# Attention over a graph: V as the stationary operand in two column halves, with probabilities normalised before they are transposed

## The chip, the cores and the metric

The kernel runs on one core of one Trainium2 chip. Times are device microseconds (us) of the core, from the first to the last instruction of one execution. The engines are PE (TensorE: products and transposes), PEld (PE's weight loads), DVE (VectorE), ACT (ScalarE), POOL (GpSimd) and SP (it issues the transfers).

## The reference, cut to what matters

Two layers of masked attention with residual and layer norm, in float32, over 128 batches of 128 tokens of 512 features. Layer 0 has 4 heads of 64, layer 1 has 8, and layer 1 normalises its input first.

```
sim  = einsum('bhid,bhjd->bhij', q, k) * scale      # layer 0: 4 heads; layer 1: 8 heads
sim  = where(mask, sim, neg)
attn = softmax(sim)                                 # over the last axis
out  = einsum('bhij,bhjd->bhid', attn, v)           # "attended values"
x    = layernorm(x + merge_heads(out) @ Wo + bo)
```

## The kernel before: the parts that matter

Four batches make a group, and there are 32 groups. A group's inputs are transposed and projected together to Q, K and V (PE alone). Then its four batches pass through five attention stages, one turn per batch; in one turn different batches stand in different stages. Layer 0 of group g alternates with layer 1 of group g - 1. A scheduler in the build decides the order on each engine from this program order.

```python
def scores(l, g, b):        # cut: products q k, masking on DVE, maximum on DVE
    for s in range(2):
        for k in range(H // 2):          # one exponential per head, on ACT, with its sum
            nc.scalar.activation(sm[:, s, k, :], sm[:, s, k, :], AF.Exp, bias=nmax[:, s, k:k + 1],
                                 accum_out=total[:, s, k:k + 1])

def probs_t(l, g, b):
    rec = three.tile([P, H // 2, 2], F32, ...)
    nc.vector.reciprocal(rec.rearrange("p k s -> p s k"), SUM[l, g, b])
    pT = two.tile([P, H, N], F32, ...)
    for h0 in range(0, H, 4):
        pt = tr_tile(...)                # a PSUM bank
        for h in range(h0, h0 + 4):      # exponentials, not yet divided, head by head
            nc.tensor.transpose(pt[:, (h - h0) * N:(h - h0 + 1) * N], sm[:, h % 2, h // 2, :], ident)
        ...                              # copied to pT by DVE (first four) or ACT

def attend(l, g, b):
    for h in range(H):                   # the exponentials are stationary, V moves (64 columns)
        nc.tensor.matmul(pm[:, h * D:(h + 1) * D], pT[:, h, :], v[:, b, h * D:(h + 1) * D],
                         start=True, stop=True)
    nc.vector.tensor_mul(a, pm, rec)     # cut: the division, while leaving PSUM

def attended_t(l, g, b):                 # `a` is transposed by PE, copied by ACT to aT
    ...

def residual(l, g, b):                   # cut: xb = x + bias (POOL), o = aT Wo (PE), y = o + xb, norm (DVE)
    ...

STAGES = (scores, probs_t, attend, attended_t, residual)

for g in range(NG + 1):                  # cut
    transposed(0, g, X[g]); project(0, g)
    for b in range(G):
        turn((0, g, b))
        if b == 1 and g > 0:
            h = prenorm(g - 1)           # the norm in front of layer 1
    transposed(1, g - 1, h); project(1, g - 1)
    for b in range(G):
        turn((1, g - 1, b))
```

## Time and profile before

| | before |
|---|---|
| time, median of 3 runs | 4096.69 us (4096.34 to 4097.61) |
| one group of four batches, from the trace | 126.28 us |
| of it layer 1: projections / attention | 42.43 / 30.03 us |
| of it layer 0: projections / attention | 21.08 / 32.74 us |
| PE idle in the profiled run | 4094.8 - 3890.9 = 203.9 us |

The group is cut where an attention stretch starts (the first output product `o` after the V projection) and where a projection starts (the first product `qk`). The prediction below cuts one stretch a little later, so its rows differ by one or two us.

### The profile page before, as it was taken

The numbers are of one execution on the slowest core, as the hardware profiler recorded it, in microseconds if no ns is written. First come the engines' busy times: TensorE is split into PE (matmuls) and PEld (weight loads), VectorE is DVE, ScalarE is ACT, GpSimd is POOL, SyncE is SP. The second block draws the span as 40 slices with busy tenths as digits, with TensorE's granted clock in tenths as the row PEclk, the third lists the DMA queues.
The fourth block names the chain that finished last, engine by engine and source line by source line (L and its number), as shares of the span: only waits on it lengthen the run. The fifth ranks groups of instructions, "written<-read, shape, count | busy, mean of one in ns | idle before, by whom it ended". The sixth has DMA issues, their size and how long they took to land.

```text
span 4094.8 us, 42881 instructions
## 1 busy us (share of the span) xinstructions
PE 3890.9 (95%) x16193; PEld 2270.6 (55%) x16193; DVE 1654.0 (40%) x3366; ACT 1139.0 (28%) x4013; POOL 755.3 (18%) x1095
## 2 busy tenths in 40 slices
PE   8999999999999999999999999999999999999998
PEld 5555555555555555555555555555555555555554
DVE  3343443434434334334344343443434434334443
ACT  2322322223323133232232222322313323223222
POOL 1121211212212112112121121221211211112120
PEclk8999999999999999999999999999999999999998
DMA  3000000000000000000000000000000000000000
GB/s 100 12 22 11 22 17 17 22 11 22 22 14 19 16 17 22 17 17 22 11 22 17 16 22 11 22 19 14 22 11 22 22 14 19 21 12 22 6 13 14
DMA packets 56894, 78.78 MB, mean 19 GB/s; under 512 B 19816, under 2 KB 21360, under 8 KB 56688
## 3 DMA queue, kind: packets, MB, share of 16 engines
q1 hardware_dynamic: 56688, 76.04, 5.4%
q8 instruction: 128, 2.10, 0.2%
q14 instruction: 78, 0.64, 0.1%
HBM read 42.47 MB, written 33.55 MB: 19 GB/s over the span
## 4 chain that ended last, share of the span: by engine, by line
PE 72%; DVE 13%; POOL 7%; ACT 4%; issue 3%; DMA 1%; POOLq 0%; ACTq 0%
PE qk L134 33%; PE v L148 16%; PE o L252 8%; PE av L211 4%; PE xt L118 3%; PE sc L170 3%; DVE sm L175 3%; ACT sm L182 3%; PE pt L196 3%; POOL rstd L239 3%; POOL xb L249 2%; DVE nmax L178 2%; POOL sm L173 2%; DVE h L271 1%; DVE y L255 1%
## 5 line engine op out<-in xcount | busy, mean ns | idle before, releaser
L134 PE MATMUL qk<-xT,w 128*128 128x512 f32 x3072 | 1364.2, 601 | 0.0
L134 PEld LDWEIGHTS qk<-xT,w 128*128 128x128 f32 x3072 | 582.1, 193 | 674.9 <-issue 665.1
L249 POOL TENSOR_TENSOR xb<-x,bias 128x512 f32<-128x512 f32 x256 | 324.4, 1267 | 2776.4 <-DVE x L255 1577.2
L252 PE MATMUL o<-wo,aT 128*128 128x512 f32 x1536 | 768.3, 630 | 2.6 <-ACT aT L226 1.8
L182 ACT ACTIVATE sm<-sm,nmax 128x128 f32<-128x128 f32 x1536 | 595.0, 390 | 462.5 <-DVE nmax L178 461.4
L148 PE MATMUL v<-w,xT 128*128 128x256 f32 (+1 forms) x2048 | 670.9, 486 | 0.0
L148 PEld LDWEIGHTS v<-w,xT 128*128 128x128 f32 x2048 | 389.1, 190 | 285.0 <-issue 260.2
L141 DVE COPY qk<-qk 128x512 f32<-128x512 f32 x96 | 66.4, 692 | 959.5 <-PE qk L134 959.5
L196 PE MATMUL pt<-ident,sm 128*128 128x128 f32 x1536 | 317.9, 306 | 124.5 <-ACT sm L182 122.3
L150 DVE COPY v<-v 128x512 f32<-128x512 f32 x192 | 132.8, 692 | 747.4 <-PE v L148 747.4
L226 ACT COPY aT<-at 128x256 f32<-128x256 f32 (+1 forms) x256 | 121.8, 476 | 1117.1 <-PE at L224 1116.6
L252 PEld LDWEIGHTS o<-wo,aT 128*128 128x128 f32 x1536 | 288.3, 203 | 253.4 <-issue 230.8
L211 PE MATMUL av<-v,pT 128*128 128x64 f32 x3072 | 378.2, 274 | 0.2 <-DVE pT L202 0.2
L211 PEld LDWEIGHTS av<-v,pT 128*128 128x128 f32 x3072 | 369.6, 195 | 1.2 <-DVE pT L202 0.9
L196 PEld LDWEIGHTS pt<-ident,sm 128*128 128x128 f32 x1536 | 202.0, 154 | 272.9 <-ACT sm L182 188.5
L170 PE MATMUL sc<-qk 64*128 64x128 f32 x3072 | 319.4, 299 | 1.7 <-DVE sm L175 1.7
L175 DVE COPY_PREDICATED sm<-m,sc 128x256 f32<-128x256 uint8 (+1 forms) x512 | 283.0, 574 | 39.1 <-PE sc L170 35.8
L182 ACT ACTIVATION_READ_ACCUMULATOR sm<-sm,nmax 128x1 f32 x1536 | 289.8, 189 | 0.0
L170 PEld LDWEIGHTS sc<-qk 64*128 64x128 f32 x3072 | 233.7, 187 | 57.4 <-issue 27.8
L173 POOL MEMSET sm<- 128x512 f32 (+1 forms) x256 | 197.9, 773 | 301.9 <-PE pt L196 301.6
L178 DVE TENSOR_REDUCE nmax<-sm 128x4 f32<-128x512 f32 (+1 forms) x256 | 240.8, 940 | 3.3
L137 ACT ACTIVATE qk<-qk 128x512 f32<-128x512 f32 x192 | 114.6, 597 | 424.5 <-PE qk L134 424.5
(45 smaller groups left out, 2217.4 us busy)
## 6 DMA issues: line engine op xcount, KB each, us to landing
x<-in_x_dram SPq DMA_DIRECT2D x32, 1024.0 KB, 5.3
out_dram<-y SPq DMA_DIRECT2D x128, 256.0 KB, 2.0
w_qkv<-in_L_gnn_w_qkv_dram SPq DMA_DIRECT2D x12, 256.0 KB, 2.7
m<-in_adj_dram SPq DMA_DIRECT2D x32, 64.0 KB, 2.1
w_out<-in_L_gnn_w_out_dram SPq DMA_DIRECT2D x4, 256.0 KB, 2.7
w<-in_L_gnn_Wq_dram SPq DMA_DIRECT2D x1, 512.0 KB, 6.4
w<-in_L_gnn_Wk_dram SPq DMA_DIRECT2D x1, 512.0 KB, 7.3
w<-in_L_gnn_Wv_dram SPq DMA_DIRECT2D x1, 512.0 KB
```

The costliest lines, as they stand in the source:

```text
L134: nc.tensor.matmul(pm, W[l][:, c, f * P:(f + 1) * P], xT[:, c, :], start=(c == 0), stop=(c == KC - 1))
L148: nc.tensor.matmul(pm[:, (b - b0) * I:(b - b0 + 1) * I], xT[:, c, b * N:(b + 1) * N], W[l][:, c, 2 * I:3 * I], start=(c == 0), stop=(c == ...
L150: nc.vector.tensor_copy(v[:, b0:b0 + per, :], pm.rearrange("p (b i) -> p b i", i=I))
L170: nc.tensor.matmul(ps[:, h % 2, h // 2, :], qk[r, h // 2, t], qk[r, H // 2 + h // 2, t], start=True, stop=True)
L173: nc.gpsimd.memset(sm, (NEG0, NEG1)[l])
L175: nc.vector.copy_predicated(sm[:, s], mask[:, None, :].to_broadcast([P, H // 2, N]), ps[:, s, :H // 2, :])
L178: nc.vector.tensor_reduce(nmax, sm, AX.X, ALU.max, negate=True)
L182: nc.scalar.activation(sm[:, s, k, :], sm[:, s, k, :], AF.Exp, bias=nmax[:, s, k:k + 1], accum_out=total[:, s, k:k + 1])
L196: nc.tensor.transpose(pt[:, (h - h0) * N:(h - h0 + 1) * N], sm[:, h % 2, h // 2, :], ident)
L211: nc.tensor.matmul(pm[:, h * D:(h + 1) * D], pT[:, h, :], v[:, b, h * D:(h + 1) * D], start=True, stop=True)
L249: nc.gpsimd.tensor_tensor(xb, xin, (bias0, bias1)[l], op=ALU.add)
L252: nc.tensor.matmul(pm, aT[:, c * P:(c + 1) * P], WO[l][:, c, :], start=(c == 0), stop=(c == nk - 1))
```

## The change

V becomes the stationary operand, so the product comes out transposed already: heads with even numbers write PSUM partitions 0 to 63, heads with odd numbers 64 to 127 (two column halves of the array). The transposes of attended values, `attended_t`, go. But queries now lie along the free axis, so the division by the row sum can no longer be done there; it moves ahead of the transposes of the probabilities, half of the heads on POOL and half on DVE.

```diff
     def probs_t(l, g, b):
-        rec = three.tile([P, H // 2, 2], F32, ...)
-        nc.vector.reciprocal(rec.rearrange("p k s -> p s k"), SUM[l, g, b])
+        rec = three.tile([P, 2, H // 2], F32, ...)
+        nc.vector.reciprocal(rec, SUM.pop((l, g, b)))
+        for s, eng in enumerate((nc.gpsimd, nc.vector)):
+            eng.tensor_tensor(sm[:, s], sm[:, s],
+                              rec[:, s, :, None].to_broadcast([P, H // 2, N]), op=ALU.mult)
 ...
     def attend(l, g, b):
         for h in range(H):
-            nc.tensor.matmul(pm[:, h * D:(h + 1) * D], pT[:, h, :], v[:, b, h * D:(h + 1) * D], ...)
-        nc.vector.tensor_mul(a, pm, rec)
-    def attended_t(l, g, b): ...
+            r = slice((h % 2) * D, (h % 2 + 1) * D)
+            nc.tensor.matmul(pm[r, h // 2 * N:(h // 2 + 1) * N], v[:, b, h * D:(h + 1) * D],
+                             pT[:, h, :], ...)
+        nc.scalar.copy(aT, pm[:, :I // P * N])
 ...
-    STAGES = (scores, probs_t, attend, attended_t, residual)
+    STAGES = (scores, probs_t, attend, residual)
```

More of the change, by code (lines that the diff above doesn't have):

```diff
@@ L151, in project @@
         QK[l, g], V[l, g] = qk, v
-    SM, PT, SUM, A, AT = {}, {}, {}, {}, {}
+    SM, PT, SUM, AT = {}, {}, {}, {}
     def scores(l, g, b):
@@ L188, in probs_t @@
         sm = SM.pop((l, g, b))
-        rec = three.tile([P, H // 2, 2], F32, tag="rec", name=f"rec{l}_{g}_{b}")
-        nc.vector.reciprocal(rec.rearrange("p k s -> p s k"), SUM[l, g, b])
-        SUM[l, g, b] = rec
+        rec = three.tile([P, 2, H // 2], F32, tag="rec", name=f"rec{l}_{g}_{b}")
+        nc.vector.reciprocal(rec, SUM.pop((l, g, b)))
+        for s, eng in enumerate((nc.gpsimd, nc.vector)):
+            eng.tensor_tensor(sm[:, s], sm[:, s],
+                              rec[:, s, :, None].to_broadcast([P, H // 2, N]), op=ALU.mult)
         pT = two.tile([P, H, N], F32, tag="pT", name=f"pT{l}_{g}_{b}")
@@ L207, in attend @@
         pT, v = PT.pop((l, g, b)), V[l, g]
-        rec = SUM.pop((l, g, b)).rearrange("p k s -> p (k s)")
         pm = mm_tile(f"av{l}_{g}_{b}")
         for h in range(H):
-            nc.tensor.matmul(pm[:, h * D:(h + 1) * D], pT[:, h, :], v[:, b, h * D:(h + 1) * D],
-                             start=True, stop=True)
-        a = two.tile([P, I], F32, tag="a", name=f"a{l}_{g}_{b}")
-        nc.vector.tensor_mul(a.rearrange("p (h d) -> p h d", d=D),
-                             pm[:, :I].rearrange("p (h d) -> p h d", d=D),
-                             rec[:, :, None].to_broadcast([P, H, D]))
-        A[l, g, b] = a
-    def attended_t(l, g, b):
-        I = INNER[l]
-        a = A.pop((l, g, b))
-        pt = tr_tile(f"at{l}_{g}_{b}")
-        for c in range(I // P):
-            nc.tensor.transpose(pt[:, c * P:(c + 1) * P], a[:, c * P:(c + 1) * P], ident)
-        aT = two.tile([P, I], F32, tag="aT", name=f"aT{l}_{g}_{b}")
-        nc.scalar.copy(aT, pt[:, :I])
+            r = slice((h % 2) * D, (h % 2 + 1) * D)
+            nc.tensor.matmul(pm[r, h // 2 * N:(h // 2 + 1) * N], v[:, b, h * D:(h + 1) * D],
+                             pT[:, h, :], start=True, stop=True)
+        aT = two.tile([P, I // P * N], F32, tag="aT", name=f"aT{l}_{g}_{b}")
+        nc.scalar.copy(aT, pm[:, :I // P * N])
         AT[l, g, b] = aT
```

## The prediction

> **What bounds the kernel now.** I read the busy line of the page first, then the chain that ended last, then busy time by stretch of one group of four batches, then the groups by shape, last the timeline of TensorE (PE).
>
> ```profile
> PE 3890.9 (95%) x16193; PEld 2270.6 (55%) x16193; DVE 1654.0 (40%) x3366; ACT 1139.0 (28%) x4013; POOL 755.3 (18%) x1095
> ...
> PE 72%; DVE 13%; POOL 7%; ACT 4%; issue 3%; DMA 1%; POOLq 0%; ACTq 0%
> ```
>
> PE is busy for 95% of the span, yet only 72% of the chain lies on it; 24% lies on DVE, POOL and ACT. So some stretches are tied to PE's work and others to a chain over the other engines, which PE happens to fill. One group shows which (columns: stretch, its length, then busy us of PE, PEld, DVE, ACT, POOL, the clock, DMA):
>
> ```profile
> 1503.10:1545.50 42.40, 42.40 (x102) 18.90 (x101) 3.75 (x7) 6.74 (x17) 0.00 (x0) 0.98 0.00 0
> 1545.50:1577.00 31.50, 29.22 (x186) 20.32 (x185) 23.38 (x44) 15.47 (x66) 11.05 (x16) 0.95 0.12 36
> 1577.00:1596.60 19.60, 19.60 (x63) 11.62 (x62) 1.59 (x3) 4.33 (x14) 0.00 (x0) 1.00 0.00 1
> 1596.60:1629.40 32.80, 29.59 (x160) 19.45 (x159) 22.75 (x52) 8.80 (x31) 12.54 (x18) 0.97 0.08 32
> ```
>
> A group takes 126.3 us. Rows one and three are the projections of layer 1 and layer 0: PE alone, 62 us, untouched by the change. Rows two and four, 64.3 us, are attention, and there DVE is busy for 46.1 us (72%). Everything the change touches lies in these two rows. PE's only large wait is there too:
>
> ```profile
> PE pt L196 <- ACT sm L182: 122.3, 93, 2.6
> ```
>
> 122 of PE's 204 idle us (4094.8 - 3890.9) are transposes of probabilities waiting for their exponentials.
>
> ```profile
> 1548.87 1.16 PE L170 MATMUL sc<-qk 64*128 64x128 f32 x16
> 1549.96 1.98 PE L252 MATMUL o<-wo,aT 128*128 128x512 f32 x4
> ...
> 1567.18 0.63 PE L224 MATMUL at<-ident,a 128*128 128x128 f32 x4
> 1567.65 1.90 PE L211 MATMUL av<-v,pT 128*128 128x64 f32 x16
> 1569.48 1.16 PE L170 MATMUL sc<-qk 64*128 64x128 f32 x14
> ```
>
> From start to start: 4 transposes `at` take 0.47 us (0.12 each), 16 `av` passes 1.83 us (0.114 each), 16 score passes 1.09 us (0.068 each, entry and exit included). Every float32 product is two passes: 3072 `av` records for 12 heads x 128 batches = 1536 products.
>
> **What the Trainium skill says.** "TensorE: Matmul & The Clock Gate", section LDWEIGHTS, gives a weight load as columns / 1.2 ns, so 107 ns for 128 columns. The trace agrees: `av` moves only 64 columns and still takes 114 ns a pass, so it is paced by its 128-column load. "TensorEngine Tiling (Array Packing)", Key Properties, says that tiles load and multiply in parallel, and that changing the tiling mode drains the engine. Scores agree on both: two heads in the two row halves take 0.068 us a pass where untiled passes take 0.11, and entering and leaving costs more than a plain step. No run here shows column tiles in float32. "GPSIMD Engine Reference", Specifications, says that GpSimd shares its SBUF interfaces with VectorE and contends with DVE instructions of two SBUF inputs; this trace has almost none of those, so it does not show it, but the change adds one beside each new POOL multiply. "VectorE: DVE Perf Modes", the section on the errata, gives a float32 tensor_tensor as (N+151)/0.96 ns: 691 ns for 512 elements, against 680 here for the old multiply out of PSUM.
>
> **The change, part by part.**
>
> ```profile
> L211 PE MATMUL av<-v,pT 128*128 128x64 f32 x3072 | 378.2, 274 | 0.2 <-DVE pT L202 0.2
> L182 ACT ACTIVATE sm<-sm,nmax 128x128 f32<-128x128 f32 x1536 | 595.0, 390 | 462.5 <-DVE nmax L178 461.4
> L249 POOL TENSOR_TENSOR xb<-x,bias 128x512 f32<-128x512 f32 x256 | 324.4, 1267 | 2776.4 <-DVE x L255 1577.2
> L224 PE MATMUL at<-ident,a 128*128 128x128 f32 x768 | 129.5, 278 | 0.1
> L214 DVE TENSOR_TENSOR a<-av,rec 128x512 f32<-128x512 f32 x128 | 87.0, 680 | 82.0 <-PE av L211 82.0
> ```
>
> PE loses the 768 `at` transposes: 768 x 0.117 = 90 us. `av` keeps 3072 passes, each now 64 columns of weights (53 ns) and 128 moved (107 ns, two halves at once if tiles overlap as in scores): 3072 x (0.114 - 0.06) = 166 us less. If the halves do not overlap, a pass is about 0.107 and 20 us are saved. Mode changes: counted in the order of the built kernels, 884 before and 950 after, as the new order splits fewer score batches; 66 x about 0.1 = 7 us. PE work falls by about 250 us, 7.8 us a group. ACT keeps its 256 copies of `aT`, now straight out of `av`. DVE swaps its multiply out of PSUM (680 and 410 ns) for one of half the probabilities (the same 512 or 256 elements): nothing. POOL gains 128 x 1.27 + 128 x 0.65 = 246 us (755 to 1000) and has room.
>
> The cost is in the order of things. Before, a transpose needed only its own head's exponential, so the first one started 0.55 us after the first exponential (1554.42 to 1554.97). Now it needs all exponentials of the batch (8 x 0.385 = 3.1 us in layer 1, 4 x 0.385 = 1.5 in layer 0, by start to start in the timeline), the reciprocal (0.2), and POOL's multiply (1.27 or 0.65): 4.6 and 2.4 us from the first exponential. The first transpose of a batch moves back by 4.0 and 1.8 us, the last by some 1.6 and 1.0.
>
> So I walked one group by hand through the built order of each engine, with the durations of these rows and 0.6 us from start to start for a DVE instruction of 512 elements.
> Layer 1's attention, from the end of its projections: the scores of batch 0 end at 4.1, their masking on DVE comes behind a normalisation of layer 0 and ends at 7.0, the maximum at 8.2, exponentials at 11.4; the reciprocal stands on DVE behind the next batch's masking and maximum and ends at 13.3, POOL's multiply at 14.7. PE has run out of other work at 11.5: an idle 3.2 us where before 1.1 were lost. Batches 1 and 2 then go at ACT's and DVE's pace: transposes at 20.3 and 26.3. The next group's input transposes start near 28.0; before, 28.2 (1545.56 to 1573.77).
> Layer 0's attention: DVE makes `h` from 20.8 to 22.7, frees the transposed probabilities of batch 1 at 23.4, masks batch 2 by 25.0, maximum 26.2, exponentials 27.9, multiply 28.8; PE idles from 24.1 to 28.8. Before, that transpose stood at 29.2 (1596.67 to 1625.84).
> Sum: 0.2 + 0.4 = 0.6 us a group, x 32 = 19 us. Of PE's 7.8 us a group, some 7 come back as waits.
>
> **The rivals.** (1) PE's saving is kept: 7.8 us x 32 = 250 us off, 3850 us. For it speak the 95% of PE and the small waits in its groups; against it, the chain's 24% on other engines and DVE's 72% in attention, which would be 46 of 56 us, in strict order. A half-way outcome, idle growing by 4 us a group, gives 3975.
> (2) The waits overtake the saving: DVE's and POOL's multiplies contend and each takes half as long again, 0.6 us for four batches of layer 1 and 0.3 for four of layer 0, about half of it on the chain: 1.8 us a group, 4135 us.
> (3) The column halves do not overlap, or their loads are not hidden: 5 us more PE work a group, largely into the new idle time; 1 to 2 us on the path, 4110 to 4140.
>
> **Range and chances.** The walk gives 4097 - 19 = 4078. Its errors, some 1 us a stage, repeat in all 32 groups and so do not average out: about 45 us. Rival 1 pulls down further than 2 and 3 push up, so I put the time at 4065 us, with 3975 to 4135 as the range. Faster by over 2% (below 4015) needs at least 2.5 us a group to survive: 0.20. Slower by over 2% (above 4178) needs contention and failed overlap together: 0.05. Within 2%: 0.75.
>
> **What would show it.** PE's busy time falls to about 3650 us (89 to 91%) while its idle time at the transposes of probabilities grows from 122 to 300 us or more, now ended by POOL's multiply rather than by ACT. No `at` group; 16 `av` passes from start to start in 1.0 to 1.3 us (overlap) or 1.8 (none). The projections keep 42.4 and 19.6 us. POOL near 1000 us with its new multiply at 1.27 and 0.65 us; DVE near 1650. The chain that ended last gains shares of ACT, DVE and POOL and loses some of PE's 72%. I am wrong if the idle time at the transposes stays below 200 us, for then the scheduler's order hides the longer chain and the time goes to 3900 or below; wrong the other way if the POOL or DVE multiply takes far longer than these rows say.

## The result, and the profile after

The changed kernel is correct and takes 4289.71 us (median of 4 runs, 4288.20 to 4292.08) against 4096.51 us for the kernel before: ratio 1.0473 with a 95% interval of 1.0458 to 1.0487. It is slower by 4.7%, and the time lies above the predicted range of 3975 to 4135 us. Ratios here and below are the mean of one kernel's fast runs over the mean of the other's in the same rounds, so they are not quite the ratio of the medians quoted.

The page of the changed kernel, its busy line and the summary of the chain that ended last:

```profile
PE 3696.3 (86%) x15425; PEld 2032.8 (47%) x15425; DVE 1758.0 (41%) x3366; ACT 1166.6 (27%) x4013; POOL 1024.0 (24%) x1351
...
PE 67%; DVE 15%; POOL 12%; issue 5%; ACT 1%; DMA 1%; POOLq 0%; ACTq 0%
```

PE works 195 us less than before but is idle for 4286.4 - 3696.3 = 590 us instead of 204. POOL's share of the chain rises from 7% to 12%.

One group of the changed kernel by stretch (length, then busy us of PE, PEld, DVE, ACT, POOL, then PE's mean clock, DMA share, GB/s):

```profile
1573.58:1616.00 42.42, 42.42 (x102) 18.87 (x102) 3.46 (x5) 5.29 (x9) 0.00 (x0) 0.98 0.00 0
1616.00:1650.12 34.12, 26.54 (x174) 17.28 (x172) 26.05 (x45) 17.62 (x73) 16.76 (x20) 0.85 0.13 41
1650.12:1671.26 21.14, 21.14 (x70) 12.62 (x70) 1.38 (x2) 2.95 (x5) 0.00 (x0) 1.00 0.00 1
1671.26:1706.72 35.46, 24.79 (x142) 14.44 (x141) 23.99 (x53) 10.38 (x39) 15.31 (x22) 0.88 0.06 23
```

The projections stand (42.42 and 21.14 us). Layer 1's attention grew from 30.03 to 34.12 us, layer 0's from 32.74 to 35.46. The group takes 133.14 us, 6.86 more (times 32 that is 220 us, a little over the 193 us of the whole, so this group lies slightly above the mean). PE's clock in the attention rows fell too: 0.94 and 0.97 before with the same cuts, 0.85 and 0.88 now.

The waits of PE in the changed kernel (total us, times, longest):

```profile
PE pt L199 <- POOL sm L193: 385.4, 155, 6.3
PE av L216 <- DVE pT L205: 63.7, 30, 2.4
PE o L245 <- ACT aT L219: 52.6, 66, 0.9
```

Where transposes of probabilities waited 122.3 us for exponentials, they now wait 385.4 us for POOL's multiply. Two waits that did not show before, of `av` on a DVE copy and of `o` on an ACT copy, add 116 us.

The new groups, by shape (busy us, mean ns of one, then idle of the engine before them):

```profile
L193 POOL TENSOR_TENSOR sm<-sm,rec 128x512 f32<-128x512 f32 x128 | 163.2, 1275 | 171.2 <-DVE rec L190 171.2
L193 DVE TENSOR_TENSOR sm<-sm,rec 128x512 f32<-128x512 f32 x128 | 122.7, 959 | 1.1
L193 POOL TENSOR_TENSOR sm<-sm,rec 128x256 f32<-128x256 f32 x128 | 89.4, 698 | 177.6 <-DVE rec L190 177.5
L193 DVE TENSOR_TENSOR sm<-sm,rec 128x256 f32<-128x256 f32 x128 | 73.5, 574 | 2.2
```

PE's timeline in that group (start, us, instruction, then the idle time ahead and what ended it):

```profile
1630.84 0.69 PE L199 MATMUL pt<-ident,sm 128*128 128x128 f32 x2 [2.71 <-POOL sm L193]
...
1632.19 1.54 PE L199 MATMUL pt<-ident,sm 128*128 128x128 f32 x6
...
1634.83 1.93 PE L216 MATMUL av<-pT,v 128*64 128x128 f32 x16
...
1645.65 1.09 PE L199 MATMUL pt<-ident,sm 128*128 128x128 f32 x8 [2.55 <-POOL sm L193]
...
1674.78 1.09 PE L216 MATMUL av<-pT,v 128*64 128x128 f32 x16
1675.81 1.10 PE L199 MATMUL pt<-ident,sm 128*128 128x128 f32 x8
...
1702.84 0.48 PE L199 MATMUL pt<-ident,sm 128*128 128x128 f32 x1 [5.51 <-POOL sm L193]
```

From 1674.78 to 1675.81 sixteen `av` passes take 1.03 us, 0.064 each, so the two column halves do overlap. After the 2.71 us wait the same work costs more: sixteen `av` passes 1.93 instead of 1.09 us, six transposes 1.54 us where a later six in the same stretch take 0.82. The clock record says why, in the stretch from 1629.51 on:

```profile
1629.51:1636.34 6.83, 5.50 (x34) 4.39 (x36) 5.11 (x12) 3.78 (x17) 4.43 (x5) 0.52 0.00 0
```

The clock (third number from the end) is 0.52 there. Summed over the run, half-clock stretches hold 254 us of PE's busy time before and 461 us after.

All engines' timeline in the same stretch, cut to the new multiplies and a POOL instruction:

```profile
1637.35 0.68 DVE L193 TENSOR_TENSOR sm<-sm,rec 128x512 f32<-128x512 f32 x1
...
1642.88 1.26 POOL L242 TENSOR_TENSOR xb<-x,bias 128x512 f32<-128x512 f32 x1 [1.79 <-DVE y L248]
...
1643.45 1.25 DVE L193 TENSOR_TENSOR sm<-sm,rec 128x512 f32<-128x512 f32 x1
...
1644.10 1.49 POOL L193 TENSOR_TENSOR sm<-sm,rec 128x512 f32<-128x512 f32 x1
```

The same DVE multiply takes 0.68 us when POOL has all but finished its own and 1.25 us when it runs beside POOL's `xb` and then POOL's multiply.

### The profile page after: what moved, and what is told of

Same layout as the page of the kernel before. It is cut to its first block, busy times and chain, and to the rows that moved or that the text cites. A ratio compares the mean times of both kernels' runs of the same rounds, so it can differ in the third digit from the quotient of the medians.

```text
span 4286.4 us, 41730 instructions
## 1 busy us (share of the span) xinstructions
PE 3696.3 (86%) x15425; PEld 2032.8 (47%) x15425; DVE 1758.0 (41%) x3366; ACT 1166.6 (27%) x4013; POOL 1024.0 (24%) x1351
## 4 chain that ended last, share of the span: by engine, by line
PE 67%; DVE 15%; POOL 12%; issue 5%; ACT 1%; DMA 1%; POOLq 0%; ACTq 0%
PE qk L134 31%; PE v L148 15%; PE o L245 7%; PE pt L199 5%; PE xt L118 4%; POOL sm L193 3%; POOL rstd L232 3%; POOL xb L242 3%; DVE sm L175 3%; DVE nmax L178 3%; PE sc L170 2%; DVE st L224 2%; DVE h L264 2%; PE av L216 2%; POOL sm L173 2%
## 5 line engine op out<-in xcount | busy, mean ns | idle before, releaser
L242 POOL TENSOR_TENSOR xb<-x,bias 128x512 f32<-128x512 f32 x256 | 338.6, 1323 | 2590.2 <-DVE x L248 1594.9
L245 PE MATMUL o<-wo,aT 128*128 128x512 f32 x1536 | 741.2, 609 | 52.7 <-ACT aT L219 52.6
L199 PE MATMUL pt<-ident,sm 128*128 128x128 f32 x1536 | 291.0, 320 | 386.2 <-POOL sm L193 385.4
L219 ACT COPY aT<-av 128x256 f32<-128x256 f32 (+1 forms) x256 | 122.1, 477 | 1248.3 <-PE av L216 1248.0
L245 PEld LDWEIGHTS o<-wo,aT 128*128 128x128 f32 x1536 | 271.4, 192 | 302.2 <-issue 215.5
L193 POOL TENSOR_TENSOR sm<-sm,rec 128x256 f32<-128x256 f32 (+1 forms) x256 | 252.5, 986 | 348.8 <-DVE rec L190 348.7
L170 PE MATMUL sc<-qk 64*128 64x128 f32 x3072 | 282.1, 313 | 31.1 <-DVE sm L175 31.1
L216 PE MATMUL av<-pT,v 128*64 128x128 f32 x3072 | 251.4, 305 | 63.9 <-DVE pT L205 63.7
L216 PEld LDWEIGHTS av<-pT,v 128*64 128x64 f32 x3072 | 185.7, 151 | 223.6 <-issue 97.5
L170 PEld LDWEIGHTS sc<-qk 64*128 64x128 f32 x3072 | 216.2, 202 | 113.3 <-issue 54.3
```

What stands on the lines that cost most here:

```text
L170: nc.tensor.matmul(ps[:, h % 2, h // 2, :], qk[r, h // 2, t], qk[r, H // 2 + h // 2, t], start=True, stop=True)
L193: eng.tensor_tensor(sm[:, s], sm[:, s], rec[:, s, :, None].to_broadcast([P, H // 2, N]), op=ALU.mult)
L216: nc.tensor.matmul(pm[r, h // 2 * N:(h // 2 + 1) * N], v[:, b, h * D:(h + 1) * D], pT[:, h, :], start=True, stop=True)
L242: nc.gpsimd.tensor_tensor(xb, xin, (bias0, bias1)[l], op=ALU.add)
L245: nc.tensor.matmul(pm, aT[:, c * P:(c + 1) * P], WO[l][:, c, :], start=(c == 0), stop=(c == nk - 1))
```

## The experiments

Fifteen kernels ran, each with one look and three timed rounds. The expectations use letters for some theories: A is the longer chain in front of a batch's transposes; B is the multiplies as load on DVE and POOL; C is that the change takes a stage out of the pipeline; D is PE's half clock after a wait; E is the bunching of input transposes at the ends of attention. Any other rival is said in words where it stands. Medians are compared with a kernel before that stood at 4094.8 to 4097.2 us.

### 1. What each half of the change costs

**no_norm**, the changed kernel without the two multiplies (a wrong result, relative error 0.979):

```diff
-        for s, eng in enumerate((nc.gpsimd, nc.vector)):
-            eng.tensor_tensor(sm[:, s], sm[:, s], rec[:, s, :, None].to_broadcast(...), op=ALU.mult)
```

> The changed kernel without its two multiplies of the probabilities (the reciprocal stays, unused); the result is wrong on purpose. Theory A (the change loses because a transpose now waits for all exponentials, the reciprocal and the multiply of its batch): with the multiplies gone a transpose waits for its own exponential again, PE's saving of some 250 us shows, and the time is 3850 to 3930 us, PE idle at most 250 us. Theory C (the loss comes from the pipeline that is one stage shorter, now that the attended values have no stage for their transposes): the stages stay as they are, so the time stays above 4050 us.

Measured: 3977.49 us, ratio 0.9706 (0.9692 to 0.9721). Against the changed kernel, normalising ahead costs 4289.7 - 3977.5 = 312 us. V stationary without any division at all is worth 4097.2 - 3977.5 = 120 us. A's range is missed by 47 us, though the time is well below C's bound: PE is idle for 264 us, 129 of them in a new wait of the transposes, which the profile puts down to DVE's statistics for a norm and which no theory named.

**before_norm**, the kernel before with nothing but the normalisation moved ahead:

```diff
     def probs_t(l, g, b):
+        for s, eng in enumerate((nc.gpsimd, nc.vector)):
+            eng.tensor_tensor(sm[:, s], sm[:, s], rec[:, s, :, None].to_broadcast(...), op=ALU.mult)
     def attend(l, g, b):
-        nc.vector.tensor_mul(a, pm, rec)
+        nc.vector.tensor_copy(a, pm[:, :I])
```

> The kernel before with the normalisation moved ahead of the transposes and nothing else: products and transposes of attended values as before, a plain copy in place of the multiply. The result is right. Theory A: it loses all of what the changed kernel loses and has none of PE's saving, or the same group time as the changed kernel since waits set it: 4250 to 4400 us. Theory C: five stages as before, so little is lost: below 4170 us.

Measured: 4524.24 us, ratio 1.1045 (1.1029 to 1.1062). That is above A's range and far from C's. Normalising ahead costs 427 us here. With it in place, V stationary is worth 4524 - 4290 = 235 us. So the product part does what it was made for, and the normalisation takes back more.

### 2. The dependency, or the multiplies as load

**scratch**, the changed kernel with both multiplies kept but writing to a tile that nobody reads, so that the transposes take the raw exponentials (a wrong result):

```diff
+        scratch = two.tile([P, 2, H // 2, N], F32, ...)
-            eng.tensor_tensor(sm[:, s], sm[:, s],
+            eng.tensor_tensor(scratch[:, s], sm[:, s],
```

> The changed kernel with both multiplies done in full on POOL and DVE, but into a tile that nobody reads; the transposes take the exponentials as they are, so the result is wrong on purpose. It has the changed kernel's work on every engine without the dependency. Against 3977 us without the multiplies and 4290 with them: if the wait for the multiply is what costs (A), it stays below 4060 us; if the multiplies cost by occupying DVE and POOL and slowing each other (B), it goes above 4150 us. In between, the two share the 312 us in that proportion.

Measured: 4047.69 us, ratio 0.9883 (0.9869 to 0.9898). PE's waits in this run:

```profile
PE pt L200 <- ACT sm L182: 175.9, 128, 2.8
PE av L217 <- DVE pT L206: 89.6, 30, 3.4
```

The time is on A's side. The load of the multiplies on DVE and POOL costs 4048 - 3977 = 70 us. Making the transposes depend on them costs the other 4290 - 4048 = 242 us: POOL's multiply no longer ends any large wait here. The builder re-orders with these edits too: compared place by place by what they write, PE's instructions differ from the changed kernel's at 2517 of 9025 places in scratch and at 2442 in no_norm. So the 242 us are the dependency together with the order that the builder makes of it.

**own_stage**, the changed kernel with reciprocal and multiplies in a stage of their own, one turn ahead of the transposes:

```diff
-    STAGES = (scores, probs_t, attend, residual)
+    STAGES = (scores, normalise, probs_t, attend, residual)
```

> The changed kernel with the reciprocal and the multiplies in a stage of their own, one turn ahead of the transposes; the work is the same, instruction for instruction. Theory A: the longer chain is given a turn's time, so PE's waits at the transposes of probabilities fall from 385 us to below 200 and the time to 3900 to 4050 us. Theory B (the multiplies on DVE and POOL themselves cost the time, by slowing each other and standing in the way in their queues): the multiplies are all there, so the time stays at 4150 us or above.

Measured: 4083.99 us, ratio 0.9968 (0.9953 to 0.9983), correct. Moving the same instructions a turn earlier wins 206 us. PE's waits came out as A said, the time 34 us above its range and below B's. What PE waits for now:

```profile
PE pt L202 <- POOL sm L192: 85.4, 36, 2.6
PE xt L118 <- DVE pT L208: 77.5, 30, 2.6
PE xt L118 <- ACT xT L120: 70.3, 30, 2.3
```

The wait on POOL fell from 385 to 85 us, but 148 us of new waits stand at the transposes of a group's inputs (`xt`), which come in a bunch at the end of each attention stretch.

### 3. Fewer stages, other engines, another buffer

**empty_stage**, an empty stage before `residual` (and a third `aT` buffer for it), to give the pipeline its fifth stage back without moving the multiplies:

```diff
-    STAGES = (scores, probs_t, attend, residual)
+    STAGES = (scores, probs_t, attend, lambda *_: None, residual)
```

> The changed kernel with an empty stage where the transposes of attended values had stood, so that the output projection of a batch comes as late in the pipeline as before (and one more buffer for its input). Theory C (a shorter pipeline is the cause): below 4170 us. Theory A: the transposes of probabilities stand as close behind their scores as in the changed kernel, so 4230 to 4330 us.

Measured: 4343.50 us, ratio 1.0607 (1.0589 to 1.0624), slower still and 13 us above A's range. The number of stages is not what was lost; theory C falls.

**dve_heads**, the multiplies on DVE alone, one per head, with a reciprocal per half, so that a transpose needs only its own head:

```diff
-        for s, eng in enumerate((nc.gpsimd, nc.vector)):
-            eng.tensor_tensor(...)
+        for s in range(2):
+            nc.vector.reciprocal(rec[:, s], total[:, s])
+            for k in range(H // 2):
+                nc.vector.tensor_scalar(sm[:, s, k, :], sm[:, s, k, :], rec[:, s, k:k + 1], None, op0=ALU.mult)
```

> The changed kernel with the normalisation head by head on DVE (two reciprocals of half the heads, then one tensor_scalar of 128 elements for each head) and none on POOL. Theory A: the chain from the first exponential to the first transpose is shorter by the multiply of half a batch and half of the exponentials, some 2.5 us in layer 1, and the waits fall to about 250 us; but DVE has some 1 us more work for each batch of layer 1. I expect 4050 to 4180 us. Theory B: no multiply on POOL and no DVE instruction with two SBUF inputs, so nothing slows anything: below 4050 us.

Measured: 4449.54 us, ratio 1.0861 (1.0843 to 1.0879), far outside what was expected. Its DVE multiplies, by shape:

```profile
L194 DVE TENSOR_SCALAR sm<-sm,rec 128x128 f32<-128x128 f32 x1536 | 361.7, 285 | 6.6
```

At 285 ns each, eight heads are 2.3 us on DVE, and the transposes wait 358 us for them. Finer pieces hardly shortened the wait. That this is because DVE, busy for 1880 us here against 1758, is the wrong queue for them is argued and not shown.

**mul_dve**, both multiplies of a batch on DVE, whole:

```diff
-        for s, eng in enumerate((nc.gpsimd, nc.vector)):
+        for s, eng in enumerate((nc.vector, nc.vector)):
```

> The changed kernel with both multiplies of a batch on VectorE and none on GpSimd; the builder's order of the engines moves with it. Contention as the main cost: the multiplies take about 0.68 us each in layer 1 instead of 0.96 and 1.28 on average, the waits of the transposes shrink, 4100 to 4220 us. The order as the main cost (VectorE's queue now carries 256 us more and the transposes wait for its end in place of GpSimd's): 4260 to 4420 us.

Measured: 4393.60 us, ratio 1.0728 (1.0712 to 1.0744). Its waits and its multiplies:

```profile
PE pt L199 <- DVE sm L193: 260.7, 215, 3.7
PE pt L199 <- POOL ve L230: 78.6, 30, 2.6
PE pt L199 <- DVE mv L225: 65.1, 30, 2.2
```

The transposes wait 404 us in all, now for DVE and for what stands in DVE's queue. The time lies in the range of the order as the main cost. A 512-element multiply still takes 876 ns on average: 194 of the 256 take 0.65 to 0.69 us, and the 62 that start while POOL runs an instruction of its other work take 1.17 to 1.76 us. The order of PE differs from the changed kernel's at 870 of 9025 places, so this is not a clean measure of contention, but taking the multiply off POOL is no cure.

**xb3**, a third buffer for `xb`, in case POOL's queue is held up by its `xb` instructions (the orders of PE, DVE and ACT are unchanged):

```diff
-        xb = two.tile([P, E], F32, tag="xb", ...)
+        xb = three.tile([P, E], F32, tag="xb", ...)
```

> The changed kernel with a third buffer for the sum of input and bias, which POOL computes; the order of PE, DVE and ACT is the same, instruction for instruction. In the trace of the changed kernel POOL's multiply of the third batch of layer 1 stands behind such a sum, which waits for DVE to free its buffer. If this standing in the queue is a part of the loss, 1 us a group or some 30 us are won: 4240 to 4270 us. If not, within 10 us of the changed kernel's 4290.

Measured: 4289.53 us, ratio 1.0475 (1.0460 to 1.0491). No effect.

### 4. The half clock

**filler_l1**, two products whose result is overwritten, put ahead of the transposes of the third batch of layer 1, where PE waits 2.55 us:

```diff
+FILL = {(1, 2): 2}
+            if h0 == 0 and (l, b) in FILL:
+                for _ in range(FILL[l, b]):
+                    nc.tensor.matmul(pt, ident, WO[l][:, 0, :], start=True, stop=True)
```

> The changed kernel with two useless products of 128x512 (1.7 us of PE at full clock) ahead of the transposes of the third batch of layer 1, where PE waits 2.55 us for POOL in each group; they write the bank that the transposes then overwrite, so the result is right. The order is the same but for the fillers and small moves of ACT. Theory D (idle PE loses half of its clock for some us after such waits, and that is a part of the loss): 55 us of added work make the kernel faster, by 10 to 50 us, 4240 to 4280 us, and the half clock after this wait is gone from the records. If the clock does not matter: 4290 or slower, up to 4310.

Measured: 4291.17 us, ratio 1.0478 (1.0463 to 1.0494). The added work is absorbed, and nothing is won. The half-clock stretch behind this wait went, but another appeared, and PE's busy time in half-clock stretches was 497 us against 461.

**filler_l0**, five such products in layer 0's 5.51 us wait, written behind the score products of the fourth batch (the orders of DVE, ACT and POOL are unchanged):

```diff
+FILL = {(0, 3): 5}
+        if (l, b) in FILL:
+            pf = mm_tile(...)
+            for _ in range(FILL[l, b]):
+                nc.tensor.matmul(pf, ident, WO[l][:, 0, :], start=True, stop=True)
```

> Five extra products of 0.86 us each at full clock stand in PE's 5.5 us wait before the transposes of the third batch of layer 0; the orders of DVE, ACT and POOL are unchanged. They add some 138 us of PE work. Theory D (PE runs at half its clock for a while after a long idle, and this is part of the loss): the 10.2 us half-clock stretch behind that wait goes, some 2 us a group are won, 4200 to 4260 us. If the half clock costs nothing because the other engines pace that stretch anyway: 4280 to 4300 us. If the wait is not filled and the products simply add: 4400 us or more.

Measured: 4298.56 us, ratio 1.0497 (1.0479 to 1.0515), 9 us more than the changed kernel. D's number is missed; the time is that of the case in which the half clock costs nothing, but the trace does not bear that reading out. One line of its waits says that the products did fall into a wait:

```profile
PE pt L204 <- POOL sm L198: 235.6, 140, 2.7
```

It fell by 150 us from 385. But half-clock stretches hold 522 us of PE work now, more than the 461 without filler, for in 15 of the 32 groups most of the filler itself ran in one. The two cases can be told apart group by group. From the end of one V projection of layer 1 to the next, a group of the changed kernel takes 133.1 us. With the filler at full clock it takes 131.8 to 131.9 us, with most of it at half clock 134.0 to 134.8 us. The stretch before the first of these groups holds two fillers and is 10 us longer than in the changed kernel. So where the filler kept full clock 1.2 us a group were won, in D's direction, and the total hides it.

The cost of the half clock by itself can be read from two groups of one trace, since PE has the same instructions in the same order in each. Here are an early and a later group of own_stage (columns as in the table by stretch):

```profile
153.34:276.80 123.46, 114.40 (x481) 61.79 (x481) 52.77 (x105) 35.42 (x125) 30.78 (x42) 0.96 0.05 18
780.61:906.91 126.30, 117.22 (x482) 63.08 (x481) 53.71 (x105) 35.19 (x125) 30.86 (x42) 0.93 0.05 18
```

PE is idle for 9.1 us in both, but 9.9 us of its busy time lie in half-clock stretches in the first and 15.7 us in the second, which is 2.84 us longer: about half of the 5.8 us. Two groups of the changed kernel differ in the same way: 132.11 and 133.12 us, 18.2 us idle in both, 11.5 and 13.8 us at half clock. The same shows in part 3: dve_heads, mul_dve and empty_stage take longer than the changed kernel although PE is idle for less (569, 563 and 554 us against 590); its busy time in half-clock stretches is 743, 677 and 645 us against 461.

### 5. PE's other work spread over the waits

In the kernel before and in the changed one, a group's 16 input transposes come together at the end of an attention stretch. Three kernels give them out in chunks of four, one after each attention turn: those of layer 0 over the preceding turns of layer 1, those of layer 1 over the second to fourth turn of layer 0.

```diff
             for b in range(G):
                 turn((0, g, b))
-                if b == 1 and g > 0:
-                    h = prenorm(g - 1)
+                if g > 0:
+                    if b == 0:
+                        h = prenorm(g - 1)
+                    else:
+                        transposed(1, g - 1, h, ((0,), (1,), (2, 3))[b - 1])
 ...
             for b in range(G):
                 turn((1, g - 1, b))
+                if g + 1 < NG:
+                    transposed(0, g + 1, X[g + 1], (b,))
```

This is the advice of the Trainium skill in "Perfetto Trace Analysis", section Optimization Strategy: where a kernel has stretches with different limits, interleave them.

**before_spread**, this edit on the kernel before:

> The kernel before with the same spreading of input transposes and nothing else, to tell what spreading alone is worth. PE is busy for 95% of the span there, so at most its waits and half clock at the stage ends can go: 4000 to 4100 us. If it falls as far as spread does, the gain is the spreading's and the change has no part in it.

Measured: 3940.05 us, ratio 0.9627 (0.9613 to 0.9641), more than I had thought possible. PE's idle time fell from 204 to 117 us and its busy time in half-clock stretches from 254 to 86 us, so a tuned kernel with PE at 95% still had 155 us in the order of its work.

**after_spread**, this edit on the changed kernel:

> The changed kernel with the same spreading and nothing else. Theory A (the dependency of a batch's transposes on the multiplies of the same turn sets the pace): the wait of the transposes of probabilities on POOL stays above 250 us and the time stays at 4200 to 4300 us. Theory E alone (stage ends matter, the dependency doesn't): 4000 to 4100 us.

Measured: 3949.30 us, ratio 0.9643 (0.9628 to 0.9657). Neither theory had this right. The wait on POOL is still there:

```profile
PE pt L200 <- POOL sm L194: 229.2, 131, 3.4
```

It stays near the 250 us that A asked for, yet the time went below 4000 us. It is level with before_spread: the change's loss of 193 us is 9 us in this order.

**spread**, this edit and own_stage together:

> own_stage (normalisation one turn ahead of the transposes) plus the transposes of a group's inputs given out chunk by chunk between the attention turns before them. Theory E (what keeps own_stage at 4084 us are the waits of input transposes on DVE and ACT copies at the ends of the attention stages, about 148 us, and the half clock behind them): 3850 to 4000 us, and the two waits of xt fall below 40 us together. If those waits only move to the next product: within 1% of 4084 us.

Measured: 3836.38 us, ratio 0.9368 (0.9354 to 0.9382), correct. Its busy line and PE's two largest waits:

```profile
PE 3611.5 (94%) x15425; PEld 1938.4 (51%) x15425; DVE 1700.3 (44%) x3365; ACT 1132.1 (30%) x4014; POOL 977.3 (25%) x1351
```

```profile
PE pt L203 <- POOL sm L193: 93.8, 46, 2.8
PE xt L120 <- DVE h L268: 65.9, 31, 7.4
```

PE is at 94% again, with 279 us less work than before. This kernel beats both, and beats before_spread by 104 us, so the change pays once the order suits it (no further order was tried for the kernel before). The time is a little below the range that E gave. The `xt` waits on copies fell from 148 to 13.5 us, as E had it, but a new one, on the normalised input `h`, took 66.

**no_norm_spread**, after_spread without the two multiplies (a wrong result; the edit is that of no_norm):

> after_spread without the two multiplies (a wrong result on purpose). It gives what normalising ahead costs when PE's other work is spread, against 312 us in the unspread order. If spreading hides most of it: 3820 to 3900 us (50 to 130 us below after_spread). If the cost is as before and spreading won elsewhere: about 3640 us. V stationary alone would then be worth the difference to before_spread's 3940 us, 120 us in the unspread order.

Measured: 3859.11 us, ratio 0.9425 (0.9411 to 0.9439). It lies in the first of the two ranges: normalising ahead costs 3949 - 3859 = 90 us in this order instead of 312.

**spread2**, layer 1's input transposes after the third and fourth turn of layer 0 in place of the second to fourth:

```diff
-                    else:
-                        transposed(1, g - 1, h, ((0,), (1,), (2, 3))[b - 1])
+                    elif b > 1:
+                        transposed(1, g - 1, h, ((0, 1), (2, 3))[b - 2])
```

> spread with the inputs of layer 1 transposed after the third and fourth turn, two chunks each, in place of the second to fourth. The wait of input transposes on the normalised input (66 us, and half clock behind it) should go below 20 us: 3740 to 3800 us. If the work that is moved leaves a hole at the second turn instead: 3820 to 3860 us.

Measured: 3834.65 us, ratio 0.9365 (0.9349 to 0.9380), the same as spread, and within the range of the hole that only moves. The waits show the trade:

```profile
PE xt L120 <- DVE pT L209: 91.8, 40, 2.8
```

The wait on `h` fell to 7.4 us, as expected, and this wait on a DVE copy came in its place.

### What the runs add up to

| us, medians | inputs bunched | inputs spread |
|---|---|---|
| kernel before | 4097 | 3940 |
| V stationary, no normalisation (wrong result) | 3977 | 3859 |
| V stationary, normalised in the turn of the transposes (the change) | 4290 | 3949 |
| V stationary, normalised one turn ahead | 4084 | 3836 |

Down a column, V stationary gives 120 or 81 us, normalising ahead takes 312 or 90, and doing so one turn earlier gives back 206 or 113.

## Why the prediction was wrong

**What bounds the kernel.** The reading was right: the attention rows are where the change is decided, and the projections did not move.

**PE's saving: right in kind, its size not measured closely.** There are no `at` transposes any more, `av` runs at 0.064 us a pass (predicted 0.06, halves overlapping), and rival 3 is out. PE's busy time is 3696 us and not the 3650 predicted; part of it now runs at half clock. Taking half of PE's busy time in half-clock stretches as lost, an estimate from the clock record that fits the two groups of own_stage in part 4, leaves 3891 - 127 = 3764 us of work before and 3696 - 231 = 3465 after: 299 us less, where 250 was predicted. The estimate is rough: no_norm has the changed kernel's instructions on PE, and by the same rule it has 3711 - 129 = 3582 us of work, only 182 us less than before. The terms of the prediction's sum, with the measured 0.064, give 90 + 154 = 244 us.

**"Sum: 0.2 + 0.4 = 0.6 us a group": this step failed.** The walk had the attention stretches slightly shorter; they are 4.09 and 2.72 us longer. Its first position held: the transposes of layer 1's first batch start 14.84 us after the projections (14.7 in the walk). From there it drifted:

| us from the end of the projections | walk | measured |
|---|---|---|
| layer 1, second batch | 20.3 | 22.5 |
| layer 1, third batch | 26.3 | 29.7 |
| layer 1, next input transposes | 28.0 | 31.4 |
| layer 0, `h` finished | 22.7 | 24.7 |
| layer 0, third batch | 28.8 | 31.6 |

The two stretch ends are late by 3.4 and 2.8 us, 6.2 us a group; over 32 groups that is 198 of the 212 us between the walk's 4078 and 4290. The runs say which kind of cost was missing. Of the 312 us of normalising ahead, 242 are the dependency and 70 the load. The walk knew the chain, but it drew every position from uncontended durations and from a PE at full clock. Half clock shows before the second batch already: from the first batch's transposes on PE had five pieces of work that took 6.2 us, where pieces of these sizes take 3.5 us at full clock elsewhere in the group. POOL's multiply for the second batch ended at 21.5 us, past the walk's 20.3 too; in front of its reciprocal DVE had stood for 1.15 us waiting for POOL's part of a norm. That each lateness then feeds the next batch, because the transposes, their copies and the products of one batch stand in the same queues as the masking of the next, is argued and not shown.

**"DVE swaps its multiply ... nothing": mis-sized.** The new DVE multiplies take 959 and 574 ns on average where 680 and 410 were carried over: 122.7 + 73.5 us against 87.0 + 128 x 0.41, which is 57 us more. DVE is at 1758 us and not near 1650. Most of the new multiplies stand behind a POOL instruction, as the last section shows. POOL's side was right: 1275 and 698 ns, 1024 us in all.

**Rival 2, "the waits overtake the saving": the right rival, mis-sized.** It was given 1.8 us a group beyond the walk; the time came out 212 / 32 = 6.6 us a group beyond it. The DVE multiplies do take some 40% longer, POOL's on average 1275 ns, as the walk had them. Contention is seen in the durations; scratch puts what it and the other load cost without the dependency at 70 us, in its own order of the engines, but how much of the 242 us would go if DVE and POOL did not slow each other was not separated, since no kernel here takes away the contention alone.

**The half clock was in no step.** In the accounts of the two traces PE's work fell by 299 us, its idle time rose by 386, and the estimated clock loss by 104: together +191, the difference of the spans (4286.4 - 4094.8), as it must be. So about a fifth of what came back, 104 of 490, was in no step at all; the fifth is as rough as the estimate of the work. That the half clock costs time by itself, and is not only an echo of the waits, is shown by the groups of equal idle time in part 4. How much of the 193 us would go without it was not measured, since neither filler rid the kernel of it.

**"Some 7 come back as waits."** By the same rough accounts 15.3 us a group came back, (386 + 104) / 32, against 9.3 us of work saved.

**The condition that I had not seen.** The prediction asked how long the chain is, and not what PE could do meanwhile. The input transposes were free to fill those waits and stood in a bunch behind them. Spread out, PE's idle time in the changed kernel falls from 590 to 332 us and its half-clock work from 461 to 255 us, and the same chain, with 229 us of waits on POOL still to be seen, costs the change only 9 us. The builder re-orders all engines with that edit, so this is a result for the order as a whole and not for one wait.

**The signs that were named.** Idle at the transposes over 300 us and ended by POOL: yes, 385.4. More of the chain on DVE and POOL: yes, 15% and 12%; more on ACT: no, from 4% to 1%. The stated way of being wrong, multiplies far longer than the rows say, is at most a part of what came: DVE's took 40% longer, POOL's did not.

## What to carry to other kernels

When a change saves work on the busiest engine by lengthening the chain in front of it, ask first what that engine can do during the chain; if nothing independent is placed there, the saving comes back as waits. Put a step that was moved ahead into a pipeline stage of its own, a turn earlier than its reader, and hand out bunched independent work between the turns. A hand walk with uncontended durations was right here for its first position only: allow for contention and for the clock behind each new wait.

## What the Trainium skill lacked or had wrong

- "TensorE: Matmul & The Clock Gate", section HAM oscillation: its rule is "no PE-idle gaps >~3.4µs". The length of the stretches agrees (3.41, 6.83 and 10.24 us, at a mean clock near 0.5), but here the clock halved behind shorter waits: 2.71 and 2.55 us in the changed kernel, and 1.11 us in the kernel before, where a half-clock stretch began 0.9 us behind it. No single length is the limit: after the first 150 us of four traces (before, changed, own_stage, spread) 182 of the 183 waits of 2.5 to 3.5 us had a half-clock stretch begin in them or within 1.8 us, but in spread only 21 of the 31 waits of 1.6 to 2.5 us did. The page's next section says that short idle times between groups of products do it too, but names no length.
- "GPSIMD Engine Reference", Specifications, names the contention with VectorE but no size, and "VectorE: DVE Perf Modes", the section on the errata, gives 691 ns for such an instruction with no word of a neighbour on POOL; the mean here was 959 ns. The size is not lacking in the skill, though: "SBUF — State Buffer", section SBUF: two separate sides, says that whichever starts first has the shared ports for its whole instruction and the other waits. The trace agrees: of the 128 DVE multiplies of 512 float32 in the changed kernel, 96 start while a POOL instruction that reads is running, and each ends 0.55 to 0.57 us after that one ends; the other 32 take 0.69 us. POOL's own took 1.04 to 1.55 us.
- "TensorEngine Tiling (Array Packing)", Key Properties, leaves open whether float32 products overlap in column tiles. They do: 0.064 us a pass for 64 columns of weights and 128 moved, in two halves, against 0.114 untiled.
